# New turns for the list scheduler of a 16-sequence hybrid block

## The chip, the cores and the metric

The kernel runs on one core of a Trainium2 chip. The metric is the device time of one execution in microseconds. A core has a matmul engine (PE, with its weight loads shown apart as PEld), a vector engine (DVE), a scalar engine (ACT), a general engine (POOL), and SP, which here only issues DMA transfers. Each of the five works through its own list of instructions in order; they wait for one another by semaphores.

## The reference

The input is 16 sequences of 512 rows with 256 features. Each goes through four layers, each added to its own input: attention, a routed feed-forward layer, a state-space layer, and the same routed layer again. Everything is 32-bit floating point.

```python
x = x + attention(layernorm(x))     # rms norm, 16 heads of 16, causal softmax; gives norm + out
x = x + ffn(layernorm(x))           # routed: 6 experts of rank 16, best 2 by softmax
x = x + ssm(layernorm(x))
x = x + ffn(layernorm(x))

def ssm(x):                         # 16 states per feature
    xc = silu(conv4(x) + conv_b)    # causal, per feature
    delta = softplus(xc @ Wd.T + bd)
    h_t = exp(A * delta_t) * h_{t-1} + delta_t * xc_t * B_t     # B = xc @ Wb.T
    y_t = sum over states of h_t * C_t                          # C = xc @ Wc.T
    return (y * sigmoid(x @ Wg.T + bg)) @ Wo.T + bo

def ffn(x):
    return x @ base_W.T + base_b + shared_B @ shared_A @ x + sum over the best 2 of w_e * routed_B_e @ routed_A_e @ x
```

## The kernel before

The work is written down as operations, 376 for each sequence and 6016 in all (1520 on PE, 1632 on DVE, 1616 on ACT, 608 on POOL, 640 DMA issues on SP). An operation is a small group of instructions of one engine with an estimated cost, the buffers it reads and writes, and sometimes an ACT table. The class `Plan` then simulates five engines: whenever an engine is free, it picks among its ready operations the one with the smallest turn whose buffers can still be had. The turn is `STARTS[sequence] + TURNS[index in the sequence]`. What it picks, in that order, is what the kernel emits, with the scheduler of the framework switched off (`manual_schedule`). So the four constants at L22 to L50 decide the order on every engine, and which earlier tile a new tile takes its place from:

- `STARTS` and `TURNS` make the turns.
- `OVER` is how far another operation may run past the time for which an engine is kept for a hand-over (a score matmul to its reduction or exponential, and from that back to PE).
- `CHANGE` is added to the turn of an ACT operation that needs another table than the one loaded.

Buffers come in small numbers, and a tile waits until the tile before it in its slot is done. PSUM has slots "one" (128x512) and "sc" (128x4x512). There are four buffers for x, so four sequences are in flight; "bc" (the B and C rows, broadcast to 128 partitions) has one.

A sequence's operations, with the lines by which the profile names them:

- *Norm*: `stats` on DVE (L481 and L482, into st and mv), `scales` on POOL (L487 to L490, into rs and nm), four scalings on ACT (L494, into xhA or xhR), a turn on PE (L505, four transposes with ident into a "one" slot), a copy on ACT (L508, into xtA or xtR).
- *Attention*: projections wq and wk (PE L474), each followed by two biased copies on ACT (L626, into qT and kT). Score matmuls (`four`, PE L566 with the mask at L568) into an sc slot. A first pass finds the largest score: reduction on DVE (L637, into negm; its four shapes have 512, 1024, 1536 and 2048 columns), a turn of negm on PE (L645), and qm on DVE (L650). A second pass has scores, an exponential on ACT (L585, into pt), and `weigh` on PE (L590, four of 128 to 512 columns that add up in one "one" slot). Then a copy avs (ACT L596), its turn `back` (PE L601) and a division (DVE L609).
- *Routed layer*: low-rank and router products (PE L474, low), the routing on DVE (L711 to L745), a turn (PE L754, hsc to hT, copied by ACT L758), and the output projection (PE L474, base with xtR, then up with hT), which DVE adds to x (L528).
- *State-space layer*: bias add on POOL (L533), convolution on DVE (L780) in a "one" slot, sigmoid, and xc (DVE L785). Projections wg, wd and wbc (PE L474). dt (softplus) and dx (DVE L817) are written to DRAM (SP L816, L819; the B and C rows at L829) and fetched back broadcast, as the scan needs them: bc (SP L830), and two fetches for each dd pair (SP L849, dd<-drows). A pair's scan is a multiply with B on POOL (L856), two exponentials on ACT (L861, into "one" slots), two scans on DVE (L864), and a multiply with C on POOL (L867). Sixteen pairs make 32 multiplies. Two pairs are summed over states by one state add on PE (L874, ysel); after four of these the gate multiply on DVE (L880) frees the slot of the sum.

SP issues transfers in its order: loads of x, rows to DRAM, bc, dd and output stores, all in one queue.

## Time and profile before

| | us |
|---|---|
| median of three runs | 2061.71 |
| the three runs | 2060.84, 2061.71, 2065.83 |
| the profiled execution | 2066.51 |
| its span | 2064.7 |
| granted PE clock, mean over the span | 0.954 |

The profiled execution lies 4.8 us above the median; 1.8 us of it are outside the span. The page gives the busy time of each engine, the span in forty slices with the granted clock of PE, the DMA queues, and groups of instructions with the idle time before them and what ended it. In a timeline, a row has its start and duration in us, the engine, the line, the operation with output and inputs, and in brackets the idle time of the engine ahead of it with what ended that. The output stores of the first thirteen sequences land at 399.8, 515.4, 630.3, and so on up to 1785.7 us.

### The profile page before, as it was taken

The page shows a single profiled execution, that of the slowest core. Times are in us where ns is not written, and L with a number is a line of the kernel's source. Part 1 is how long each engine was busy: PE and PEld are TensorE (multiplying, and loading weights), DVE is VectorE, ACT ScalarE, POOL GpSimd, SP SyncE. Part 2 cuts the span into 40 slices and gives each one's busy share as a digit, 9 for nine tenths or more (in the row PEclk, how much of TensorE's full clock was granted, in tenths as well). Part 3 has the DMA queues.
Part 4 walks back from the last instruction along what each step waited for, and adds up shares of the span by engine and source line. Part 5 has one row for each costly group of instructions (what it writes and reads, how often), then busy time and mean ns, then how long its engine had stood idle before and what let it go on. Part 6 is the DMA issues. An engine that isn't in the chain of part 4 may idle for free. (4 is left out here: it accounts for less than half of the span.)

```text
span 2064.7 us, 34733 instructions
## 1 busy us (share of the span) xinstructions
PE 1801.9 (87%) x13253; PEld 953.8 (46%) x13253; DVE 1513.4 (73%) x2479; ACT 1194.0 (58%) x1685; POOL 1371.1 (66%) x814
## 2 busy tenths in 40 slices
PE   4788789999999999999999999999999999996455
PEld 2244344555455454545455454545554454544123
DVE  4335677878788787878788787878788787876563
ACT  2236556565666757565666667575666766564431
POOL 3001784949587685859597785859596785848693
PEclk8789899999999999999999999999999999998766
DMA  3000956848494866847494867849493957747791
GB/s 93 1 1 22 216 122 155 197 127 210 109 233 109 216 164 167 205 137 191 110 231 100 225 153 175 204 120 212 110 231 95 228 143 186 183 125 183 186 222 31
DMA packets 113064, 316.35 MB, mean 153 GB/s; under 512 B 17809, under 2 KB 36610, under 8 KB 112898
## 3 DMA queue, kind: packets, MB, share of 16 engines
q1 hardware_dynamic: 112194, 313.99, 62.5%
q8 instruction: 105, 1.72, 0.4%
q14 instruction: 61, 0.50, 0.1%
q10 hardware_dynamic: 704, 0.14, 0.0%
HBM read 287.87 MB, written 26.21 MB: 152 GB/s over the span
## 5 line engine op out<-in xcount | busy, mean ns | idle before, releaser
L864 DVE TENSOR_TENSOR_SCAN dd<-one,dd 128x512 f32<-128x512 f32 x512 | 607.9, 1212 | 185.2 <-ACT one L861 88.3
L856 POOL TENSOR_TENSOR dd<-dd,bc 128x1024 f32<-128x1024 f32 x256 | 603.6, 2361 | 194.0 <-DMA dd<-drows 156.8
L867 POOL TENSOR_TENSOR dd<-dd,bc 128x1024 f32<-128x1024 f32 x256 | 601.9, 2358 | 86.2 <-DVE dd L864 80.4
L637 DVE TENSOR_REDUCE negm<-sc 128x4 f32<-128x512 f32 (+3 forms) x256 | 380.4, 1486 | 154.0 <-PE sc L568 153.7
L861 ACT ACTIVATE one<-dd,am 128x512 f32<-128x512 f32 x512 | 344.3, 689 | 249.4 <-DVE dd L864 108.9
L585 ACT ACTIVATE pt<-sc 128x2048 f32<-128x2048 f32 (+3 forms) x256 | 316.3, 1235 | 189.0 <-PE sc L568 187.8
L487 POOL TENSOR_SCALAR rs<-mv 128x4 f32<-128x4 f32 x64 | 12.3, 193 | 364.2 <-DVE mv L482 361.4
L566 PE MATMUL sc<-qm,kT 32*128 32x512 f32 (+3 forms) x2048 | 214.1, 488 | 37.8 <-ACT pt L585 28.4
L566 PE MATMUL sc<-kT,qT 32*128 32x128 f32 (+3 forms) x2048 | 217.0, 494 | 30.5 <-DVE negm L637 25.9
L568 PEld LDWEIGHTS <-identb 128*128 128x128 bf16 x2048 | 117.4, 98 | 232.4 <-issue 217.2
L874 PE MATMUL one<-dd,ysel 128*32 128x512 f32 x1024 | 172.7, 633 | 55.5 <-POOL dd L867 46.4
L590 PE MATMUL one<-pt,vv 128*32 128x512 f32 (+3 forms) x2048 | 191.6, 449 | 8.1 <-DVE dd L864 7.9
L566 PEld LDWEIGHTS sc<-qm,kT 32*128 32x128 f32 x2048 | 80.9, 185 | 181.5 <-ACT pt L585 120.4
L474 PE MATMUL one<-base,xtR 128*128 128x256 f32 x512 | 139.5, 395 | 18.6 <-DVE dd L864 18.0
L566 PEld LDWEIGHTS sc<-kT,qT 32*128 32x128 f32 x2048 | 82.0, 187 | 156.8 <-DVE negm L637 63.3
L494 ACT ACTIVATE xhR<-x,nm,rs 128x256 f32<-128x256 f32 x192 | 99.4, 588 | 53.2 <-POOL nm L490 53.1
L528 DVE TENSOR_TENSOR x<-one,x 128x512 f32<-128x512 f32 x128 | 86.4, 675 | 34.7 <-PE one L474 34.5
L474 PEld LDWEIGHTS one<-base,xtR 128*128 128x128 f32 x512 | 94.5, 194 | 36.8 <-DVE dd L864 21.5
L481 DVE BATCH_NORM_STATS2 st<-x 128x6 f32<-128x256 f32 x256 | 103.7, 405 | 4.8 <-DMA x<-in_x_dram 4.1
L568 PE MATMUL sc<-mask_q,identb 128*128 128x128 bf16 x1024 | 103.7, 225 | 0.0
L568 PE MATMUL sc<-mask_k,identb 128*128 128x128 bf16 x1024 | 102.8, 224 | 0.0
L505 PE MATMUL one<-ident,xhR 128*128 128x128 f32 x384 | 61.9, 290 | 35.2 <-ACT xhR L494 27.7
(132 smaller groups left out, 2449.4 us busy)
## 6 DMA issues: line engine op xcount, KB each, us to landing
dd<-drows SPq DMA_DIRECT2D x512, 512.0 KB
x<-in_x_dram SPq DMA_DIRECT2D x16, 512.0 KB
drows<-dt SPq DMA_DIRECT2D x32, 256.0 KB
drows<-sg SPq DMA_DIRECT2D x32, 256.0 KB
bc<-brows SPq DMA_DIRECT2D x16, 512.0 KB
out_dram<-x SPq DMA_DIRECT2D x16, 512.0 KB
brows<-few SPq DMA_DIRECT2D x16, 64.0 KB
wo<-in_Wo_dram SPq DMA_DIRECT2D x2, 256.0 KB
```

The costliest lines, as they stand in the source:

```text
L474: nc.tensor.matmul(o[:, lo:hi], lhsT=lhsT, rhs=rhs, start=n == 0, stop=n == len(todo) - 1)
L481: nc.vector.bn_stats(st()[:, t, :], x()[:, t, :])
L566: nc.tensor.matmul(sc()[:, g, 0:n], lhsT=lhsT(g), rhs=rhs(g), start=True, stop=False)
L568: nc.tensor.matmul(sc()[:, g, at : at + P], lhsT=identb, rhs=mask, start=False, stop=True)
L585: o.then = op("ACT", act(G * n), lambda pt=pt, sc=sc, n=n: nc.scalar.activation(pt(), sc()[:, :, 0:n], AF.Exp), r=[sc], w=[pt], table="exp")
L590: nc.tensor.matmul(av()[rows(g), kt * P : T], lhsT=vals()[:, kt, G * j + g, :], rhs=pt()[:, g, :], start=kt == 0, stop=kt == NT - 1,)
L637: o.then = op("DVE", dve(G * n), lambda t=t, n=n, sc=sc, nm=nm, s=s: nc.vector.tensor_reduce(nm()[:, t, :, 1 - s, 0:1], sc()[:, :, 0:n], A ...
L856: op("POOL", pool(1024), lambda dd=dd: nc.gpsimd.tensor_tensor(dd()[:, :, 1, :], dd()[:, :, 1, :], both(0), ALU.mult), port=True, r=[(bc, ...
L861: op("ACT", act(512) + 0.07, lambda i=i, k=k, dd=dd, dec=dec: nc.scalar.activation(dec(), dd()[:, i, 0, :], AF.Exp, scale=am[:, k + 4 * i ...
L864: op("DVE", 1.22, lambda i=i, dd=dd, dec=dec: nc.vector.tensor_tensor_scan(dd()[:, i, 1, :], dec(), dd()[:, i, 1, :], 0.0, ALU.mult, ALU.a ...
L867: op("POOL", pool(1024), lambda dd=dd: nc.gpsimd.tensor_tensor(dd()[:, :, 1, :], dd()[:, :, 1, :], both(1), ALU.mult), port=True, r=[(bc, ...
L874: nc.tensor.matmul(sums()[rows(g), :], lhsT=ysel[:, m, :], rhs=four[g]()[:, g % 2, 1, :], start=m == 0, stop=m == 3)
```

## The change

The four constants get new values; nothing else in the code is changed. `TURNS` takes two more lines, so that every line number after it is two higher in the changed kernel.

```diff
-OVER, CHANGE = 2.3, 97.0
+OVER, CHANGE = 2.2, 380.0
 STARTS = (
-    0, 149, 234, 338, 413, 521, 619, 700, 790, 888, 996, 1074, 1174, 1263, 1369, 1447,
+    0, 388, 628, 931, 1235, 1513, 1817, 2132, 2333, 2657, 2868, 3179, 3385, 3709, 4019, 4336,
 )
 TURNS = (
-    322, 924, 785, 870, 705, 84, 602, 525, 716, 736, 780, 829, 935, 688, 816, 888, 551, 888, 569, 780, 1037,
-    1058, 780, 1053, 1052, 703, 823, 720, 796, 729, 794, 743, 758, 752, 822, 761, 826, 825, 945, 858, 844,
...
+    964, 2212, 2292, 2200, 2062, 1448, 1180, 1130, 1289, 1208, 878, 1323, 1667, 1061, 1480, 1546, 923, 1564,
+    1137, 1245, 1723, 1569, 1215, 1549, 1604, 1023, 1210, 1051, 1339, 1100, 1237, 1133, 1350, 1139, 1158,
...
 )
```

All 376 turns differ, and all are about twice as large. The operations stay the same; what changes is the order that `Plan.order()` gives. Both orders repeat from one sequence to the next in the middle of the run. These are the pieces of them that the next section speaks of, each in the order of its engine (a line number of before stands for an operation; s is a sequence, s-1 the one that started before it):

```
PE, around the second wq projection of s (weigh 512, 384, 256, 128 by their columns)
  before: weigh 512, scores, weigh 384, wq L474, scores, weigh 256, state add s-2, hsc turn s-1, scores, weigh 128, projection base,xtR s-1
  after:  scores, weigh 512, wq L474, scores, weigh 384, state add s-2, hsc turn s-1, scores, weigh 256, weigh 128, projection base,xtR s-1
DVE, around the negm reductions of s
  before: reduction L637 (2048), scan s-2, scan s-2, qm L650, qm L650, gate multiply L880 s-2, x L528 s-3
  after:  reduction L637 (2048), scan s-2, gate multiply L880 s-2, x L528 s-3, qm L650, qm L650, scan s-2
PE, around the wd projections of s-1 (scores of the first pass by their columns for all four heads; the turns L505 at the start are those of the state-space norm)
  before: scores 1024, turn L505 s-1 twice, state add s-2, scores 1536, turn L505 s+1, weigh 128, output of s-2 twice, scores 2048, back s, turn L505 s+1, wd, wbc, scores 1024, wk s+1, scores 1536, wd, oT turn s, scores 512, wg, scores 2048, turn L505 s-2, wg, turn L505 s-2, turn L645 s
  after:  scores 1536, turn L505 s-1 twice, state add s-2, scores 1024, turn L505 s+1, weigh 128, output of s-2 twice, scores 2048, back s, turn L505 s+1, wd, wbc, scores 1024, wk s+1, scores 512, oT turn s, wd, scores 1536, wg, turn L505 s-2, scores 2048, wg, turn L505 s-2, turn L645 s
DVE, the same stretch (reductions L637 by their columns)
  before: 512, division, 1024, gate multiply s-2, three L780, 1536, two L780, x L528, L780, xc, stats, xc, 2048
  after:  512 (earlier), division, 1536, gate multiply s-2, three L780, 1024, two L780, x L528, L780, xc, stats, xc, division, 2048
PE at the end, sequences 14 and 15
  before: projection base,xtR 15 twice, add 14, turn L505 15 twice, gate projection wg 15, add 14, wg 15, wd 15, wbc 15, wd 15, add 14
  after:  hsc turn 15, projection base,xtR 15 twice, add 14, turn L505 15 twice, wg 15, add 14, wg 15, wd 15, wbc 15, wd 15, add 14
POOL at the end (L856 multiply with B, L867 with C)
  before: L856 14, L867 14, scales 15, L867 14 twice, bias add 15, L856 14 three times, L867 14 three times, L856 15 twice, L867 15, scales 14
  after:  L856 14, L867 14 twice, L856 14 twice, scales 15, L867 14 twice, bias add 15, L856 14, L867 14 twice, scales 14, L856 15 twice, L867 15
```

## The prediction

> **What bounds the kernel now.** I read the page first, then stretches of the timeline by store period, then the waits of the matmul engine one by one, and last the end of the run.

> ```profile
> PE 1801.9 (87%) x13253; PEld 953.8 (46%) x13253; DVE 1513.4 (73%) x2479; ACT 1194.0 (58%) x1685; POOL 1371.1 (66%) x814
> PEclk8789899999999999999999999999999999998766
> ```

> PE is busy for 1801.9 of 2064.7 us, so 262.8 us of idle time is all that an order of the same instructions can win. The output stores lie 115.3 to 115.8 us apart from 399.8 to 1785.7 us: twelve equal periods, one sequence each. The windows view (busy time of each engine, then granted clock and DMA share) of two periods, of two pieces of the end, and of one stretch near the start:

> ```profile
> 861.30:977.00 115.70, 108.89 (x828) 57.96 (x828) 93.65 (x153) 74.09 (x106) 86.54 (x52) 1.00 0.65 169
> 1092.30:1207.90 115.60, 108.95 (x828) 58.16 (x829) 93.68 (x153) 74.18 (x106) 85.29 (x50) 1.00 0.68 170
> 1862.70:1960.00 97.30, 54.44 (x244) 30.34 (x233) 60.32 (x94) 41.65 (x62) 72.64 (x43) 0.78 0.77 184
> 1960.00:2064.70 104.70, 52.56 (x184) 27.80 (x184) 47.78 (x84) 25.87 (x44) 68.11 (x33) 0.66 0.54 128
> 42.80:66.70 23.90, 15.44 (x72) 6.45 (x76) 9.16 (x7) 2.06 (x2) 0.00 (x0) 0.50 0.00 0
> ```

> A period has PE busy 108.9 of 115.65 us at full clock: idle about 6.6 us, twelve times 79. The head (0 to 400) has about 80 us of idle PE, the end (from 1785.7) about 102. In a period PE runs in order and stops at a dozen small places, always for a PSUM slot or an operand. The largest, in the whole timeline:

> ```profile
> 868.04 1.98 PE L474 MATMUL one<-xtA,wq 128*128 128x512 f32 x4
> ...
> 870.06 1.45 ACT L626 ACTIVATE qT<-one,bq,quarter 128x512 f32<-128x512 f32 x2 [1.67 <-PE one L474]
> ...
> 871.88 0.70 ACT L861 ACTIVATE one<-dd,am 128x512 f32<-128x512 f32 x1
> ...
> 872.66 1.22 DVE L864 TENSOR_TENSOR_SCAN dd<-one,dd 128x512 f32<-128x512 f32 x1 [1.69 <-ACT one L861]
> ...
> 875.98 1.13 PE L474 MATMUL one<-base,xtR 128*128 128x256 f32 x4 [1.39 <-DVE dd L864]
> ```

> PE waits 1.39 us at 875.98, ready to multiply, until a scan (L864) leaves the "one" slot that the output projection is to use. The scan hangs on an exponential (L861), which is behind the softmax exponential and the two qT copies on ACT, and these on the wq projection of PE itself: it has made its own wait. Two more places, in PE's own timeline:

> ```profile
> 972.23 0.65 PE L645 MATMUL one<-ident,negm 128*128 128x128 f32 x4 [0.86 <-DVE dd L864]
> 973.38 1.18 PE L874 MATMUL one<-dd,ysel 128*32 128x512 f32 x8 [0.51 <-issue]
> ...
> 1016.56 1.98 PE L474 MATMUL one<-xc,wd 128*128 128x512 f32 x4 [0.47 <-DVE xc L785]
> ```

> The end is another regime: one sequence's serial chain, with the scan's POOL multiplies and DMA fetches.

> ```profile
> 1916.22 3.78 PE L474 MATMUL one<-xpad,wg 128*128 128x512 f32 x4
> 1919.93 1.16 PE L874 MATMUL one<-dd,ysel 128*32 128x512 f32 x8
> ```
> ```profile
> 1910.65 0.19 POOL L487 TENSOR_SCALAR rs<-mv 128x4 f32<-128x4 f32 x1 [1.13 <-DVE mv L482]
> ...
> 1928.36 2.35 POOL L856 TENSOR_TENSOR dd<-dd,bc 128x1024 f32<-128x1024 f32 x1 [4.33 <-DMA dd<-drows]
> ...
> 1947.17 2.35 POOL L856 TENSOR_TENSOR dd<-dd,bc 128x1024 f32<-128x1024 f32 x1 [4.72 <-DMA bc<-brows]
> ```

> The last scan begins at 1947.17, when its "bc" lands. bc has one buffer, which sequence 14 keeps until its last multiply ends at 1942.4. That multiply was late because POOL stood 4.33 us for a fetch, whose dd slot came free only when the state add at 1919.93 had read it, and the add was queued behind sequence 15's gate projection (1916.22).

> **The change, part by part.** No instruction is added or removed: same multiplies, copies, fetches. Only OVER, CHANGE, STARTS and TURNS differ, and with them every engine's order. Laid beside each other engine by engine, the two orders are periodic in the middle, so each move counts twelve times. The ACT tables change 65 times instead of 67 by the plan; a load is 1.28 us in the trace, but ACT is busy only 74 of 115.65 us: 0.

> 1. The wq projection for the second pair of qT goes one "weigh" (L590, 384 columns) earlier. That weigh takes 0.85 us, 0.78 to the next start. The copies, the exponential and the scan that the projection at 875.98 waits for start that much earlier; PE has the same work ahead of the projection. Wait 1.39 to 0.61: gain 0.78.

> 2. The state add at 973.38 takes its slot, in the old order, from the second of the two scans before it. Now a gate multiply (L880) moved ahead of the qm operations (L650) frees it, about 0.6 us sooner. Then the qm, not the slot, is next to hold PE: gain 0.43 of 0.51. The negm wait ahead of it (0.86 here, mean 0.7) stays: there too one scan follows the reduction.

> 3. Two score groups of PE (L566, 1024 and 1536 columns) change places, and their reductions on DVE (L637): the one in the middle of the convolution becomes 1.23 (the row of 1024 columns) instead of 1.75 us. xc (L785) is ready about 0.45 us earlier: gain 0.4 of 0.47.

> 4. Against these: after the wd projections the groups of 512 and 1536 columns change places too, and a turn (L505) goes ahead of the 2048 one, whose reduction (2.28 us) is the last before the negm turn: about 0.25 us of new wait, partly taken back at the next wait (mean 0.58, a weigh that waits for a slot).

> The sum is 0.78 + 0.43 + 0.4 - 0.25 = 1.36; I take 1.2, since a gain before a wait that hangs on POOL or DMA is given back. Over twelve periods 14.4 us; the ends are 0.5 and 1.7 a period, 6 and 20 us. The other dozen waits keep order and releasers: 0. On SP the x load moves behind one dd fetch (issue 0.6 us each); x is due a whole period later: 0. On POOL most moves swap the two dd pairs of one step, and norm scales (L487 to L490) move past one multiply at most (2.35 us). They are covered by some 13 us per period in which POOL waits for mv; without that cover they would delay a turn of PE by 2.35 us.

> 5. Head. Sequence 0's k and q projections go ahead of sequence 1's turn (up to 1 us); one "back" transpose (L601, 249.42), which waited 2.19 us for a scan's slot, gets one free at 245.0: 2.6 us with what follows. The rest, 246 to 345 us, is rearranged too much to follow. I take -2, with ends -9 and +5. [...] The row 42.80:66.70 has clock 0.50 over 23.90 us, and the longest wait of PE in it is 2.39 us. [...]

> 6. End. The state add of 1919.93 now stands before sequence 15's turns and gate projection, and could run near 1912. Fetch and POOL's 4.33 us wait come earlier, sequence 14 finishes its scan 6 to 8 us sooner, and with it bc. Against it, on POOL sequence 15's scales (1910.65) stand behind three more multiplies (3 x 2.35 = 7.05 us), and sequence 14's scales (1.65 us, but waiting for mv) stand before sequence 15's first multiplies instead of after. Bounds: -8 (all of the add's gain) and +6 (all of the scales' delay, nothing of the gain). The nearest row is POOL's 4.33 us wait, which goes: I take -3.

> The sum: -14.4 - 2 - 3 = -19.4 us. The profiled execution took 2066.5 us (span 2064.7 and 1.8 around it) and becomes 2047. It lies 4.8 us above the median of 2061.7, so against the median: 2061.7 - 19.4, about 2042.

> [...]

> **Rivals.** *No change that can be measured.* The POOL and DMA chain of a sequence's scan keeps its length; if it, and not PE, sets the period, the gains of 1 to 3 come back as longer waits at the state adds. For it: all 32 multiplies of a sequence are 75 us of POOL's 86, with DMA at 0.65. Against: PE's waits at the adds are 0.5 us. Then head and end alone: -5 to +3, 2057 to 2065.

> *Slower: sequence 15's scales behind three more multiplies.* Place: POOL, near 1910. Price 7.05 us, plus up to 4 for sequence 14's scales, which wait for their mv with sequence 15's multiplies behind them. Since nothing but sequence 15 is left, it reaches the end whole. It decides if sequence 14's scan finishes less than about 7 us sooner and the periods give less than their low end of 6 us: 2065 to 2073.

> *Much more gain.* Small waits of PE hang together: a slot freed earlier at one place also serves the next. If half of the 6.6 us goes, 12 x 3.3 = 40 us, with the end 43: 2020 to 2030.

> **How the numbers follow.** Likeliest, periods shorter by 0.5 to 1.7 us: chance 0.61, 2030 to 2055. No change: 0.16. Slower: 0.12. Much more gain: 0.11. This kernel can tell about 0.3% (6.2 us) from no change: 2055.5 to 2067.9 is "same". Faster is 0.61 + 0.11 and a little of the no-change case; slower 0.11. The range reaches from 2030 to 2064, leaving out the great gain and the slow case, about 2 in 10.

> **What would show it.** Periods between stores of 114.0 to 115.1 us; the wait of the base,xtR projection for a scan at 0.6 instead of 1.39; no 0.5 before the state add nor before wd. At the end POOL's wait for dd before sequence 14's last fetches gone, and the last bc landing less than 161 us after the thirteenth store. I am wrong if the periods stay at 115.6 with PE's waits in other places, or if the span from the thirteenth store to the end (279 us) grows.

## The result, and the profile after

| | before | after |
|---|---|---|
| median, us | 2061.97 (four runs) | 2031.52 (four runs) |
| profiled execution, us | 2066.51 | 2031.46 |
| its span | 2064.7 | 2029.7 |
| granted PE clock, mean | 0.954 | 0.961 |

The new order takes 0.9853 of the time (95% interval 0.9832 to 0.9875): 30.4 us less, with an interval of about 26 to 35. The forecast was 19.4 less, at 2042, in a range of 2030 to 2064, so the measured time lies near the edge of the range. The page's first lines and its row of clocks, after the change:

```profile
PE 1782.7 (88%) x13253; PEld 948.7 (47%) x13253; DVE 1504.6 (74%) x2479; ACT 1190.5 (59%) x1683; POOL 1370.9 (68%) x814
PEclk9799899999999999999999999999999999998856
```

The same 13253 matmul records, but 19 us less of PE busy: part is a shorter half-clock time near the start (the time in which the granted clock was 0.50: 51.2 us before the first store instead of 75.1), part a wait that was counted as work, shown below. Two periods between stores, by the windows view:

```profile
847.10:961.10 114.00, 107.92 (x829) 57.99 (x828) 93.13 (x152) 74.12 (x106) 84.17 (x51) 1.00 0.71 173
1074.95:1189.10 114.15, 108.00 (x830) 57.99 (x828) 93.04 (x152) 73.90 (x106) 86.06 (x51) 1.00 0.70 172
```

The stores cut the run in three. Since the half-clock time differs between profiles of one order (in the head 75.1 us in the profile of before, 61.4 in three others with that order there), I set beside it every profile of this study in which that part had the one order or the other:

| part | old order | new order | gain | forecast |
|---|---|---|---|---|
| start to first store | 399.8 (before); 392.2 to 399.8, mean 396.3 of nine | 388.8 (after); 388.8 to 389.9, mean 389.5 of three | 6.8 | 2 |
| twelve periods | 1386.0 (before, 115.50 each); 1384.7 to 1386.0, mean 1385.4 of four | 1372.9 (114.41 each); 1368.8 to 1372.9, mean 1370.4 of four | 15.0 | 14.4 |
| thirteenth store to the end | 278.9 (before); 276.5 to 280.5, mean 279.0 of seven | 268.0 (after), 269.1 and 271.8, mean 269.6 | 9.4 | 3 |

The three gains make 31.2 us. In the two profiles alone the difference is 35.0: the profile of before had the slowest head of the nine. The twelve periods gained about what was forecast. What goes beyond the forecast, some 11 us, lies in the head and the end.

PE's timeline at the places that the prediction showed:

```profile
860.07 1.13 PE L476 MATMUL one<-base,xtR 128*128 128x256 f32 x4 [0.74 <-DVE dd L866]
884.45 1.98 PE L476 MATMUL one<-xc,wd 128*128 128x512 f32 x4
...
943.74 1.06 PE L876 MATMUL one<-dd,ysel 128*32 128x512 f32 x8 [0.77 <-POOL dd L869]
...
955.50 0.66 PE L647 MATMUL one<-ident,negm 128*128 128x128 f32 x4 [0.45 <-DVE dd L866]
956.13 1.18 PE L876 MATMUL one<-dd,ysel 128*32 128x512 f32 x8
...
959.41 0.66 PE L507 MATMUL one<-ident,xhR 128*128 128x128 f32 x4 [0.60 <-DVE dd L866]
```

The output projection waits 0.74 instead of 1.39. wd and the state add behind the negm turn have no wait at all. New is a wait before a turn of xhR (959.41; mean 0.35 in the eight periods between the third and the eleventh store), again for a scan's slot. And a state add (943.74) waits 0.77 for its multiply on POOL. The same add in the profile of before:

```profile
959.35 2.19 PE L874 MATMUL one<-dd,ysel 128*32 128x512 f32 x8
```

It shows no wait there, but runs 2.19 us instead of 1.06: PE had begun on the first four of its eight matmuls, and the last four started at 960.50, when the multiply on POOL that they need had ended (at 960.44). So PE's idle time fell by only 0.5 us a period (6.7 to 6.2, the same eight periods), and its busy time by 0.7. The time covered by state adds fell by 0.6, so most of the 0.7 is this same wait, which was counted as work before.

At the end, PE and POOL:

```profile
1880.77 1.03 PE L476 MATMUL one<-base,xtR 128*128 128x256 f32 x4
1881.63 0.60 PE L476 MATMUL one<-up,hT 113*128 113x256 f32 x2
1882.16 1.07 PE L876 MATMUL one<-dd,ysel 128*32 128x512 f32 x8
1889.67 0.48 PE L507 MATMUL one<-ident,xhR 128*128 128x128 f32 x1 [6.44 <-ACT xhR L496]
```
```profile
1886.65 0.20 POOL L489 TENSOR_SCALAR rs<-mv 128x4 f32<-128x4 f32 x1
...
1903.71 2.34 POOL L869 TENSOR_TENSOR dd<-dd,bc 128x1024 f32<-128x1024 f32 x1 [3.68 <-DVE dd L866]
1913.86 0.20 POOL L489 TENSOR_SCALAR rs<-mv 128x4 f32<-128x4 f32 x1 [7.81 <-DVE mv L484]
...
1918.80 2.36 POOL L858 TENSOR_TENSOR dd<-dd,bc 128x1024 f32<-128x1024 f32 x1 [3.10 <-DMA dd<-drows]
```

The add runs 120.5 us after the thirteenth store instead of 134.1. bc's fetch is issued 146.4 us after it instead of 156.7. Sequence 15's scan then begins at 157.2 instead of 161.4, and what it waits for is now its first dd fetch, no longer bc. Its 32 multiplies take 77.3 instead of 81.5 us. So of the 10.9 us between the two ends, the earlier scan makes 4.2 and the shorter one another 4.2; the rest, some 2.5, comes behind it. Sequence 14's scales, at 1913.86, cost nothing: the multiply behind them waits another 3.10 us for its fetch.

### The profile page after: what moved, and what is told of

It reads as the page before. It is cut to its first block, busy times and chain, and to the rows that moved or that the text cites. A ratio compares the mean times of both kernels' runs of the same rounds, so it can differ in the third digit from the quotient of the medians.

```text
span 2029.7 us, 34735 instructions
## 1 busy us (share of the span) xinstructions
PE 1782.7 (88%) x13253; PEld 948.7 (47%) x13253; DVE 1504.6 (74%) x2479; ACT 1190.5 (59%) x1683; POOL 1370.9 (68%) x814
## 4 chain that ended last, share of the span: by engine, by line
PE 19%; DMA 11%; DVE 10%; POOL 6%; issue 3%; ACT 3%; SPq 1%; POOLq 0%; DVEq 0%; ACTq 0%
DMA dd<-drows 11%; PE one L476 9%; PE sc L568 4%; DVE dd L866 4%; POOL dd L869 3%; POOL dd L858 2%; DVE negm L639 2%; PE one L876 2%; PE sc L570 2%; DVE one L782 1%; PE one L592 1%; ACT one L863 1%; PE one L507 1%; DVE st L483 1%; DVE x L530 1%
## 5 line engine op out<-in xcount | busy, mean ns | idle before, releaser
L639 DVE TENSOR_REDUCE negm<-sc 128x4 f32<-128x1024 f32 (+3 forms) x256 | 380.0, 1484 | 166.0 <-PE sc L570 166.0
L876 PE MATMUL one<-dd,ysel 128*32 128x512 f32 x1024 | 166.1, 629 | 62.4 <-POOL dd L869 47.3
L592 PE MATMUL one<-pt,vv 128*32 128x512 f32 (+3 forms) x2048 | 186.5, 443 | 7.7 <-DVE dd L866 7.6
L476 PEld LDWEIGHTS one<-base,xtR 128*128 128x128 f32 x512 | 94.7, 195 | 33.3 <-DVE dd L866 20.5
```

The source lines that it names most:

```text
L476: nc.tensor.matmul(o[:, lo:hi], lhsT=lhsT, rhs=rhs, start=n == 0, stop=n == len(todo) - 1)
L592: nc.tensor.matmul(av()[rows(g), kt * P : T], lhsT=vals()[:, kt, G * j + g, :], rhs=pt()[:, g, :], start=kt == 0, stop=kt == NT - 1,)
L639: o.then = op("DVE", dve(G * n), lambda t=t, n=n, sc=sc, nm=nm, s=s: nc.vector.tensor_reduce(nm()[:, t, :, 1 - s, 0:1], sc()[:, :, 0:n], A ...
L876: nc.tensor.matmul(sums()[rows(g), :], lhsT=ysel[:, m, :], rhs=four[g]()[:, g % 2, 1, :], start=m == 0, stop=m == 3)
```

## The experiments

The periods below are means of the eight between the third and the eleventh store. In the order of before they are 115.51, and 115.43 to 115.49 in four other kernels with that order there. In the new order they are 114.31, and 114.12, 113.98 and 113.90 in three other kernels with that order there. So one and the same order varies by 0.1 to 0.4 us, and from single profiles a difference of 0.1 is not told from none. Single times are no measure of one move: the order of before ran in 2055.8 to 2068.9 us in 23 executions, and its first store alone varied by 7 us. (The single times not given below: m2b 2060.99, m3 2058.34, m4 2059.83, add_alone 2067.15, add_and_scales 2071.92, new_scales_first 2035.94 us.) The moves are put on the finished order of before: the named operations of an engine take each other's places. An operation is (sequence, number within its sequence); s runs from 4 to 13.

### One move at a time

**The wq projection earlier.**

```diff
 PE, around the second wq projection of s
- weigh 512, scores, weigh 384, wq, scores, weigh 256, add s-2, hsc turn s-1, scores, weigh 128, projection s-1
+ scores, weigh 512, wq, scores, weigh 384, add s-2, hsc turn s-1, scores, weigh 256, weigh 128, projection s-1
```

> The order of before, with one move of the new order alone, for sequences 4 to 13: on PE the second wq projection goes ahead of the 512 and 384 weighs as in the new order. Theory (each move takes its own wait away): PE's wait before the first base,xtR projection falls from 1.39 to 0.6 to 0.8 us, a period from 115.5 to about 114.8, ten periods about 6 to 8 us. Rival (the waits of a period only change places, since POOL and DMA set its length): the wait falls, others grow by as much, the period stays 115.5.

```profile
870.84 1.13 PE L528 MATMUL one<-base,xtR 128*128 128x256 f32 x4 [0.52 <-DVE dd L918]
```

The wait fell from 1.39 to 0.61 in the mean, the period to 114.76: 0.75 less, as forecast (0.78). Nothing came back elsewhere. The one time was 2055.52 us.

**The gate multiply earlier.**

```diff
 DVE, around the 2048 reduction of s
- x addition s-3, 2048 reduction, scan s-2 (299), scan s-2 (297), qm, qm, gate multiply s-2
+ scan s-2 (299), 2048 reduction, scan s-2 (297), gate multiply s-2, x addition s-3, qm, qm
```

> The order of before, with one move alone, for sequences 4 to 13: on DVE the gate multiply (L880) and the x addition go ahead of the two qm operations, and one scan of the pair before them goes ahead of the 2048 reduction. Theory: the wait of 0.50 us before the state add goes to under 0.1, the period falls by about 0.45, the whole by about 4.5 us. Rival: other waits grow by as much, the period stays 115.5.

The state add's wait went, and yet the period grew to 116.34 us (the one time: 2066.99). PE and DVE in this kernel's timeline:

```profile
968.75 1.13 PE L528 MATMUL one<-base,xtR 128*128 128x256 f32 x4 [1.27 <-DVE dd L918]
```
```profile
965.45 1.21 DVE L918 TENSOR_TENSOR_SCAN dd<-one,dd 128x512 f32<-128x512 f32 x1
967.48 1.22 DVE L918 TENSOR_TENSOR_SCAN dd<-one,dd 128x512 f32<-128x512 f32 x1 [0.81 <-issue]
968.62 2.27 DVE L691 TENSOR_REDUCE negm<-sc 128x4 f32<-128x2048 f32 x1
```

The scan that was put ahead of the reduction frees the slot of another PE operation, the output projection of the last routed layer. Its own exponential was still second on ACT, so DVE stood 0.8 us, and PE 1.27 (1.46 in the mean). Neither theory had this. The new order exchanges those two exponentials as well:

```diff
+ ACT: exponential 298 of s-2 ahead of 296
```

> As m2_gate_earlier, with its counterpart on ACT: the two exponentials (L861) ahead of the scans that were exchanged are exchanged too, as in the new order. Theory: m2_gate_earlier lost because the scan put first on DVE had its exponential second on ACT, so the output projection of the last routed layer, whose slot that scan frees, waited 1.25 us; with the exponentials exchanged that wait is under 0.2, the state add's wait stays at 0, and the period falls from 115.5 to about 115.0. Rival: the gate multiply ahead of qm delays the second pass whatever ACT does, the period stays at or above 115.5.

The period came back to 115.39. That wait is 0.56 now, not under 0.2, and the state add's is 0; the net is 0.1 us, which is not told from none. In the new order the same move stands on two more exchanges (scans 288 and 290, and their exponentials), and the projection waits about 0.2. A kernel with all of these exchanges on the order of before was not run, so that the gain of 0.43 comes with all of its counterparts is not shown.

**The groups of 1024 and 1536 columns.**

```diff
- PE: (s, 82), (s, 84)    DVE: (s, 83), (s, 85)
+ PE: (s, 84), (s, 82)    DVE: (s, 85), (s, 83)
```

> The order of before, with one move alone, for sequences 4 to 13: the score groups of 1024 and 1536 columns ahead of the wd projection, and their reductions, change places. Theory: the wait of 0.47 us before the first wd projection goes to under 0.1, the period falls by about 0.4, the whole by 4 us. Rival: the period stays 115.5.

```profile
895.13 1.98 PE L529 MATMUL one<-xc,wd 128*128 128x512 f32 x4
```

wd has no wait, the period is 114.93: 0.58 less, against 0.4 forecast.

**The groups of 512 and 1536 columns.**

```diff
- PE: 92, wd, oT turn, 88, 94, turn L505 s-2    DVE: 93, 89
+ PE: 88, oT turn, wd, 92, turn L505 s-2, 94    DVE: 89, 93
```

> The order of before, with one move alone, for sequences 4 to 13: behind the wd projections the score groups of 512 and 1536 columns change places, and a turn L505 goes ahead of the 2048 group. The prediction gave this a new wait of 0.25 us at the negm turn or the weigh behind it: period 115.7, the whole 2.5 us longer. Rival, from the trace of the new order, which shows no such wait: the period stays or falls by up to 0.1.

The period is 115.58, within what can be told of no change; no new wait at the negm turn or behind it. The loss that I had set against the gains is not there.

### Head and end by themselves

```diff
+ result = the first 890 operations of the new order, then the rest in the order of before
```

> The new order up to the first output store (890 operations), the order of before for the rest. Theory (the order itself shortens the head, by less than the 11 us that the two profiles differ by, since the profile of before had an unusually long stretch at half clock; the order of before stored first at 392.2 to 399.8 us in five profiles): first store at 388 to 391 us, periods 115.5 and the end 277 to 280 as before; the time about 6 us under before. Rival (all of the head's difference is the chance of the clock): first store spread over 388 to 400, the time within 2 us of before.

First store at 389.8, periods 115.43, end 279.6. The time was 2053.7 us, ratio to before 0.9958 (0.9949 to 0.9967): 8.7 us less. The head's half-clock time was 61.4 us in this profile, as in three profiles of the old head, which stored first at 395.2 to 397.3. At equal half-clock time the new order is thus some 6.5 us shorter: PE's idle time in the head is 76.6 us instead of 80.4, its busy time 313.2 instead of 315.9.

```diff
+ result = the first 5021 operations of the order of before, then the rest in the new order
```

> The order of before up to the twelfth store (5021 operations), the new order for the rest. Theory (the end has its own gain, from the state add ahead of sequence 15's turns and all that follows): from the thirteenth store to the end 267 to 271 us instead of 277 to 280, the time about 10 us under before. Rival (the end was shorter only since it met the chip's clock windows at another time): 276 or more.

From the thirteenth store to the end 269.1 us; the time 2052.2, ratio 0.9947 (0.9930 to 0.9965): 10.9 us less. The end has a gain of its own, whatever comes before it.

### What makes the end shorter

```diff
- PE: turn L505 15, turn L505 15, wg 15, add (14, 309)
+ PE: add (14, 309), turn L505 15, turn L505 15, wg 15
```

> The order of before with one move alone: at the end, sequence 14's third state add of its second half goes ahead of sequence 15's turns and gate projection. Theory (that add held up the fetches, POOL and bc): POOL's wait of 4.3 us for dd near 1928 goes, bc's fetch is issued 5 us or more earlier against the thirteenth store (before: 156.7 us after it), and the end falls from 277 to 280 to about 273. Rival (sequence 15's own rows come just as late, so that bc was not alone): bc earlier, the end unchanged within 1.5 us.

The end grew to 282.4 us. PE in this kernel:

```profile
1907.44 1.91 PE L928 MATMUL one<-dd,ysel 128*32 128x512 f32 x12 [1.17 <-POOL dd L921]
1916.09 1.99 PE L928 MATMUL one<-dd,ysel 128*32 128x512 f32 x4 [6.74 <-POOL dd L921]
1918.01 1.97 PE L559 MATMUL one<-ident,xhR 128*128 128x128 f32 x8
```

The add stood 6.74 us for its second multiply, and sequence 15's turns stood behind it: they began 135.0 us after the thirteenth store, against 127.4 in the profile of before. The multiply is on POOL behind sequence 15's scales. So I gave the add its counterpart there:

```diff
- POOL: scales 15, L867 14, L867 14 (308), bias add 15, L856 14, L856 14
+ POOL: L867 14 (308), L856 14, L856 14, scales 15, L867 14, bias add 15
```

> As add_alone, with its counterpart on POOL: sequence 15's scales go behind three multiplies of sequence 14 (L867, L856, L856), as in the new order. Theory, from add_alone: there the add stood 6.7 us on PE for a multiply that POOL did only behind sequence 15's scales, and held sequence 15's turns; the move on POOL that the prediction counted as a cost of up to 7 us is what lets the add run early. The add then starts by 130 us after the thirteenth store (add_alone: 133.1), PE's wait ahead of it is under 3 us, and the end is 270 to 276 us. Rival (the prediction's reading: scales later means sequence 15 later): the end is 280 or more.

That was worse still: 288.8 us. The add's multiply ended at 1912 and PE's wait was 4.96, but sequence 15's scales came at 1920.3 (139.4 us after the thirteenth store, against 124.9), since two of the multiplies ahead of them waited for fetches. And the scans of sequence 14 gained nothing by it:

```profile
1926.73 2.35 POOL L911 TENSOR_TENSOR dd<-dd,bc 128x1024 f32<-128x1024 f32 x1
1940.75 2.34 POOL L922 TENSOR_TENSOR dd<-dd,bc 128x1024 f32<-128x1024 f32 x1 [11.66 <-DVE dd L919]
```

POOL stood 11.7 us for scans, which were left behind sequence 15's work on ACT and DVE. The last of the four runs on this takes one piece out of the complete new order:

```diff
- POOL: (14, 308), (14, 312), (14, 320), scales 15
+ POOL: scales 15, (14, 308), (14, 312), (14, 320)
```

> The new order with one move undone: sequence 15's scales on POOL ahead of the three multiplies of sequence 14 again. Theory (the two moves belong together): the add on PE waits for the multiply, sequence 15's turns behind it, and the end, 268.0 us in the profile of the new order, grows by 3 to 8 us. Rival (the prediction's reading): in the new order mv is ready 2.2 us before the scales start, so the end falls by up to 2 us.

```profile
1880.34 1.05 PE L930 MATMUL one<-dd,ysel 128*32 128x512 f32 x4
1886.85 1.92 PE L930 MATMUL one<-dd,ysel 128*32 128x512 f32 x4 [5.46 <-POOL dd L923]
1892.14 0.47 PE L561 MATMUL one<-ident,xhR 128*128 128x128 f32 x1 [3.37 <-ACT xhR L550]
```

The end is 274.2 us, 2.4 to 6.2 more than in the three profiles with the new order's end. Sequence 15's scan begins 161.9 us after the thirteenth store, against 157.2 to 157.9 in those three. So undoing the move costs, by about 4 us where it acts, while the prediction counted making it as a cost of up to 7.

What the two small kernels lacked is seen in the orders themselves: the new one also has four exponentials of sequence 14 on ACT ahead of sequence 15's state-space norm and convolution, and their four scans on DVE ahead of that convolution. In the profile of before, ACT changes tables back and forth there:

```profile
1926.35 1.28 ACT L812 ACT_TABLE_LOAD   x1
1927.65 0.69 ACT L812 ACTIVATE dt<-one,bd 128x512 f32<-128x512 f32 x1
1928.35 1.28 ACT L861 ACT_TABLE_LOAD   x1
1929.65 0.69 ACT L861 ACTIVATE one<-dd,am 128x512 f32<-128x512 f32 x1
...
1930.86 1.28 ACT L812 ACT_TABLE_LOAD   x1
1932.16 0.69 ACT L812 ACTIVATE dt<-one,bd 128x512 f32<-128x512 f32 x1
1932.86 1.28 ACT L861 ACT_TABLE_LOAD   x1
```

In the new order these four exponentials are done by 1886.3, under the exponential table that was loaded. That the exponentials and scans are the missing part is read from the two traces; a kernel with all four pieces on the order of before was not run. One more difference stands untested: the new order has sequence 14's last routed layer (its norm, its routing and its additions to x) ahead of multiplies, exponentials and scans of sequence 15's first pairs, and may owe to that some of the 4.2 us by which sequence 15's scan is shorter.

### Two additions meant to beat the new order

```diff
             o.fn()
+            if o.num - first in fill:      # ten score groups of sequence 0's first passes
+                scratch, k = fill[o.num - first]
+                for _ in range(k):         # 4, 8 or 12
+                    nc.tensor.transpose(scratch()[:, 0:P], ident, ident)
...
-                    op("POOL", pool(1024), lambda dd=dd: nc.gpsimd.tensor_tensor(
+                    own_engine = ("DVE", nc.vector, dve(1024)) if b == B - 1 and g == 2 else ("POOL", nc.gpsimd, pool(1024))
+                    op(own_engine[0], own_engine[2], lambda dd=dd, e=own_engine[1]: e.tensor_tensor(
```

> The new order with two additions meant to beat it. First, ten fillers on PE in sequence 0's first passes: 4 to 12 extra transposes of ident behind a score group, into the PSUM slot that the negm turn will overwrite. Theory of the clock (a window of 3.4 us in which PE is busy too little, not an idle gap, halves the clock, and at half clock PE is part of the head's chain): the half-clock time in the head falls from 51 to under 25 us and the first store from 388.8 or 389.8 to 383 to 386. Rival (DVE's reductions set that stretch whatever the clock): half-clock time falls, first store stays within 1.5 us. Second, in sequence 15's scan every second C multiply (8 of 16) goes to DVE. Theory (32 multiplies of 2.35 us on POOL set the last scan): the end falls from 268 to 250 to 260 us. Rival (DVE and POOL hinder each other, so that a multiply on DVE costs what it saves): 265 or more.

The two parts went opposite ways. First store at 380.7 us, half-clock time of the head 23.9: the fillers pay. The end grew to 277.6 us: the multiplies on DVE do not. All together 2029.91 us, no different from the new order. The multiply's own rows:

```profile
L870 DVE TENSOR_TENSOR dd<-dd,bc x8: 1197/2446/3281, 1925.6 to 1991.3; 128x1024 f32<-128x1024 f32 x8
```

On DVE it took 1.20 us at best, 2.45 in the median, 3.28 at worst, where POOL takes 2.35; and POOL, with fewer of them, stood for dd fetches. The fillers alone:

> The new order with the ten fillers on PE alone, all multiplies on POOL again. From new_fill_and_dve (first store at 380.7 us, half-clock time of the head 23.9 us) and the end of the new order (268.0 and 269.1 us): first store 379 to 383, periods 114.2 to 114.5, end 267 to 270, time about 2022 us, that is 8 to 10 under the new order. Rival (the shift of the whole run against the clock's windows gives the gain back later): 2028 or more.

2020.75 us (five runs, 2019.8 to 2023.43), ratio to before 0.9811 (0.9797 to 0.9824), below the interval of the new order. First store at 378.3 us, periods 113.9 (0.3 less than expected), end 271.8 (some 2 us more than expected); what shifted these two, in which the order is the new one, stays open. This is the fastest of all kernels here.

## Why the prediction was right or wrong, point by point

*What bounds the kernel.* PE with its small waits, not DVE: right. Two single moves, one on PE's order alone, shortened the period by 0.75 and 0.58 us while DVE's work stayed the same.

*Steps 1 to 4.* The sum was 1.36, taken as 1.2, and the period fell by 1.09 over the twelve of the two profiles, and by 1.25 in the means of four. Step 1 held (0.78; 0.75 alone). Step 3 was mis-sized (0.4; 0.58). Step 4's loss of 0.25 was wrong; the period did not change by more than can be told. Step 2's term (0.43) was the wait of one place, not the gain of the move: alone the move cost 0.8 us, with its exponentials it gave 0.1. The new order pays for its parts with 0.35 before a turn of xhR, which I had not seen. That the errors nearly cancel is luck.

*Step 5, the head.* The direction was right, the size was not: 2 forecast, 6.8 found, inside the ends of -9 and +5. The +5 was my estimate, from the 10.24 us at half clock that begin at 213.5 in the profile of before: as much again, costing half of it. No run shows it; the half-clock time of the head was 75.1 us in the profile of before, and with the new order 51.2 (after) and 61.4 (head_new). I had stopped following the order at 246 us and put the rest at about nothing. At equal half-clock time 6.5 us are left, 3.8 of them idle time of PE, so most of the gain is the order's. Which of its moves in the head give it was not tried, and whether the 2.7 us of busy time come from the places at which half clock falls isn't settled.

*Step 6, the end.* This is the step that failed. It took the state add's place on PE as the cause (-8 at best) and POOL's new order as its price (+7). The end fell by 9.4 us where 3 were forecast. add_alone shows that the add by itself makes the end 3.4 us longer than the old order's mean, and new_scales_first that POOL's move is part of the gain, worth about 4. The estimate that the add "could run near 1912" overlooked its second multiply, which in the very profile it was read from ended at 1917.1 on POOL:

```profile
1912.43 4.66 POOL L867 TENSOR_TENSOR dd<-dd,bc 128x1024 f32<-128x1024 f32 x2
```

And bc, which was to bring the gain, was issued 10.3 us sooner, but the scan began only 4.2 us sooner, since the first dd fetch then held it. What the runs show in place of the step is that neither piece gained without the rest (282.4 and 288.8 us), while the complete order of the end gained by itself (tail_new, 269.1): there four engines together move sequence 14's last pairs ahead of sequence 15.

*The median.* I set the gain against the median and not against the profiled execution's 2066.5. Right: that profile had the slowest head of nine.

*The rivals.* "No change" fell with the single moves. "Slower" was right in its mechanism, scales behind three more multiplies, only where the scans don't move too: add_and_scales ended 9.8 us later than the old order's mean. In the new order, where they do, it was outweighed. "Much more gain" came near in its number (2020 to 2030), not in its mechanism: PE's idle time fell by 0.5 us a period and not by half of 6.6. That the time stayed inside the range owes to its width: the excess came from the head, which had been followed only in part, and from the end, whose mechanism was wrong.

## What to carry to other kernels

An order is one thing over all engines. A move on one engine takes away the wait that is seen, but its gain stands only if what feeds it on the others is ready in time. The wq projection needed nothing else; the gate multiply and the state add lost when they moved alone. So before adding up single waits, follow each operand of the moved instruction to its own queue. And compare stage by stage over several profiles: here the head of one and the same order varied by 7 us from run to run.

## What the runs showed of the hardware

```profile
41.40:44.80 3.40, 1.02 (x17) 0.55 (x13) 2.29 (x1) 0.00 (x0) 0.00 (x0) 1.00 0.02 5
44.80:65.30 20.50, 13.88 (x64) 5.63 (x60) 7.38 (x6) 1.88 (x1) 0.00 (x0) 0.50 0.00 0
```
```profile
41.40:44.80 3.40, 1.89 (x24) 1.24 (x20) 2.29 (x1) 0.00 (x0) 0.00 (x0) 1.00 0.02 5
44.80:65.30 20.50, 16.01 (x144) 8.36 (x142) 7.38 (x6) 5.69 (x5) 0.00 (x0) 1.00 0.00 1
```

In the new order PE was busy 1.02 of 3.40 us (30%), with waits of at most 2.4 us, and then had a clock of 0.50 for 20.5 us. With eight transposes more, in new_fill, it was busy 1.89 (56%), and the clock stayed at 1.00. Over the head, half-clock time fell from 51.2 to 13.7 us, and the first store came 10.5 us sooner, although the fillers add work.

The other surprise is a DVE multiply that takes 1.20 us in one place and up to 3.28 in another of the same kernel, new_fill_and_dve. DVE and POOL there:

```profile
1985.77 3.28 DVE L870 TENSOR_TENSOR dd<-dd,bc 128x1024 f32<-128x1024 f32 x1
...
1991.33 1.23 DVE L870 TENSOR_TENSOR dd<-dd,bc 128x1024 f32<-128x1024 f32 x1
```
```profile
1985.63 2.34 POOL L858 TENSOR_TENSOR dd<-dd,bc 128x1024 f32<-128x1024 f32 x1
```

The two of the eight that ran with no multiply on POOL beside them took 1.20 and 1.23 us. The five that began while one ran took 2.06 to 3.28, and each ended 1.08 us after POOL's multiply. The eighth began 0.13 us before a multiply of POOL and took 1.22; there POOL's took 3.30 instead of 2.34. So in the six overlaps of this trace the one that began second took the longer time (2.06 to 3.28 us on DVE, 3.30 on POOL). Why is not shown; no run here tried it by itself.
